# Mamba periods: D x by a diagonal on TensorE, the unscanned states' share ahead of the scans, the residual between GpSimd's products

## The chip, the cores and the metric

The kernel runs on one core of a Trainium2 chip. The metric is the device time of one execution in microseconds. The times shown are the median of three runs and their extremes; beside them stands one profiled execution, whose trace is what the profile is read from. VectorE, ScalarE, GpSimd, TensorE and SyncE are called DVE, ACT, POOL, PE and SP in the rows of the profile. Each has its own queue and works through it in order; semaphores tie the queues together.

## The reference

The input is `x`, 8 images of 128 channels by 64 x 64 pixels, in fp32. The first layer is a Mamba block over the 4096 pixels of each image, in order, with 256 inner channels and 16 states:

```
xz = x @ W_in;  xh, z = split(xz)
xh = silu(conv of two taps over the sequence(xh))
dt_low, B, C = split(xh @ W_x)               # 8, 16, 16
dt = softplus(dt_low @ W_dt + b_dt);  A = -exp(A_log)
h[t] = exp(dt[t] A) h[t-1] + dt[t] B[t] xh[t]          # per inner channel and state
y[t] = sum over states of h[t] C[t]  +  D xh[t]
y = (y * silu(z)) @ W_out
x = silu(group_norm(y)) + x
```

After it come a layer normalisation over the channels, a causal additive attention within each image (`exp` of a tanh score, divided by its sum), a second layer normalisation with a router over 64 experts, the experts themselves, and a scatter of their outputs. The change touches the Mamba block alone.

## The kernel before

The work is done in three stages, one after the other on the same core: the Mamba block (function `mamba`), the attention with the routing (`attend`), and the experts with the scatter (in `attend` too). The order of all instructions in `mamba` and `attend` is written out by hand: each engine runs its instructions in the order in which the program issues them. A semaphore wait of one instruction holds up all that stand behind it on its engine.

`mamba` cuts the sequences into chunks of 512 pixels, eight to an image, 64 in all (NC = 64, NCH = 8). The 256 inner channels are two halves of 128 partitions, so that most tiles are 128 x 2 x 512 ("pair") and most PSUM tiles 128 x 512 ("single"). Only NR = 3 of the 16 states are scanned. For the other 13 the decay is taken to be zero within a step, so that their share of y is dt xh times the sum of B C over these states: `over`. The flag that `vanish` collects tells afterwards whether that held; it did for these inputs.

The loop at line 525 runs over periods. In one period up to ten chunks are at work, each at its own stage: c1 is the chunk that is just projected, c2 has its step sizes computed, c3 is scanned, c4 is summed, gated, projected back and stored. Then eight more chunks pass, since the group norm of an image needs all of its chunks (`store`, line 420, calls `group_norm` for the last chunk of an image). c5 is normalised, c6 gets the residual added, c7 is turned to tokens by PE, c8 is layer-normalised and turned back, c9 gets the attention's vectors, c10 is saved to DRAM. Before, c6 to c10 are 12, 13, 14, 15 and 16 periods behind the newest chunk.

The steps that the change touches, by their lines before:

- `inputs` (345): five operations on DVE, each 128 x 1024. The first (L349) computes (u + 1) - 1 with a tensor_scalar; the next three (L350 to L352) correct the logarithm with it and give dt; L354 gives dx = dt xh.
- `over` (356): one matmul (L359) of the 16-row product B C with a matrix that has ones in the rows of the unscanned states, into a single PSUM tile, and L361 on DVE, which multiplies it with dx and so begins y.
- `drive` (L377): dx times B for one scanned state, on DVE. `scan` (L386): two scans of 512 on DVE, which read the decay `da` from PSUM. `outputs` (L392): the scanned state times C, for both halves, on GpSimd, into `hc`.
- `sums` (396): for each half three matmuls by the identity (L399) add up the three `hc`, and L403 on DVE adds the sum to y.
- `gated` (405): for each half y + xh D with D per partition (L408, a scalar_tensor_tensor), then times silu(z) (L411).
- `residual` (L443): o + x for one chunk, 128 x 512, on GpSimd.
- `turn` (L450, L452), `moments` (L456 to L466: the store of the turned chunk and its statistics), `tokens` (L473: four tensor_scalar of 128 x 128 on DVE, which read the turned chunk `tt` and write `tok`), `turn_back` (L482 to L485), `vectors` (L490 to L497).
- `back` (L416) and `store` (L425, L426): the projection back, its copy by ACT and its statistics on DVE.

[...]the tag "s" has two single tiles (used in turn by pbc, pdt, py, over, pt, pb, po and the group norm), px, pz and da take two each. pz is written by `gate` and by `vectors`. `tt` has one buffer. `o` has NCH + 3 = 11 buffers, `hc` 5, `hs` 4, `db` 3.

Of the kernel before, what the change touches and what calls it, by code (L numbers as in the profile page):

```python
# [9 lines left out]
F32 = mybir.dt.float32  # L10
AF = mybir.ActivationFunctionType
ALU = mybir.AluOpType
AX = mybir.AxisListType

P = 128
CH = 512
# [19 lines left out]
NR = 3  # L36
# [8 lines left out]
def fast_path(  # L45
# [24 lines left out]
    nc = tc.nc  # L70
    B = x.shape[0]
    L = x.shape[2] * x.shape[3]
    NCH = L // CH
    NB = L // P
    NQ = CH // P
    NC = B * NCH
# [4 lines left out]
    const = ctx.enter_context(tc.tile_pool(name="const", bufs=1))  # L81
# [3 lines left out]
    ident = const.tile([P, P], F32, name="ident")  # L85
# [21 lines left out]
    def halves(name, src):  # L107
        t = const.tile([P, 2], F32, name=name)
        nc.sync.dma_start(t, src.rearrange("(h p) -> p h", p=P))
        return t  # L110

    convb = halves("convb", conv_b)
    bdt = halves("bdt", b_dt)
    dskip = halves("dskip", D)

    aneg = const.tile([P, 2, NS], F32, name="aneg")
    nc.sync.dma_start(aneg, A_log.rearrange("(h p) n -> p h n", p=P))
# [5 lines left out]
    rest = const.tile([NS, P], F32, name="rest")  # L123
# [127 lines left out]
    def mamba(mw, small, psum):  # L251
# [5 lines left out]
        ch = [{} for _ in range(NC)]  # L257
        stats = {}

        def pair(tag, name, bufs):  # L260
            return mw.tile([P, 2, CH], F32, tag=tag, name=name, bufs=bufs)

        def single(name):
            return psum.tile([P, CH], F32, tag="s", bufs=2, name=name)

        def load(c):
            b, k = divmod(c, NCH)
            xt = ch[c]["x"] = mw.tile([P, 1 + CH], F32, tag="xt", bufs=3, name=f"xt{c}")
            if k == 0:
                nc.vector.memset(xt[:, 0:1], 0.0)  # L270
                nc.sync.dma_start(xt[:, 1:], xf[b, :, :CH])
            else:
                nc.sync.dma_start(xt, xf[b, :, k * CH - 1 : (k + 1) * CH])
# [67 lines left out]
        def logarithm(c):  # L341
            ln = ch[c]["ln"] = pair("ln", f"ln{c}", 1)
            nc.scalar.activation(ln, ch[c]["u"], AF.Ln, bias=1.0)

        def inputs(c):

            u, ln, dt = ch[c].pop("u"), ch[c].pop("ln"), ch[c]["dt"]
            w = pair("db", f"w{c}", 3)
            nc.vector.tensor_scalar(w, u, 1.0, -1.0, ALU.add, ALU.add)  # L349
            nc.vector.tensor_tensor(w, u, w, ALU.subtract)  # L350
            nc.vector.tensor_tensor(w, w, ln, ALU.add)
            nc.vector.tensor_tensor(dt, dt, w, ALU.add)  # L352
            dx = ch[c]["dx"] = pair("dx", f"dx{c}", 2)
            nc.vector.tensor_tensor(dx, dt, ch[c]["xc"], ALU.mult)  # L354

        def over(c):

            po = single(f"over{c}")
            nc.tensor.matmul(po, lhsT=rest, rhs=ch[c].pop("prod"), start=True, stop=True)  # L359
            y = ch[c]["y"] = pair("y", f"y{c}", 2)  # L360
            nc.vector.tensor_tensor(y, ch[c]["dx"], po.unsqueeze(1).to_broadcast([P, 2, CH]), ALU.mult)  # L361

        def vanish(c):
            for h in range(2):
# [30 lines left out]

        def sums(c, h):
            py = single(f"py{c}_{h}")
            for n in range(NR):
                nc.tensor.matmul(  # L399
                    py, lhsT=ident, rhs=ch[c]["hc", n][:, h, :], start=n == 0, stop=n == NR - 1  # L400
                )
            y = ch[c]["y"]
            nc.vector.tensor_tensor(y[:, h, :], y[:, h, :], py, ALU.add)  # L403

        def gated(c):
            y = ch[c]["y"]
            for h in range(2):
                nc.vector.scalar_tensor_tensor(  # L408
                    y[:, h, :], ch[c]["xc"][:, h, :], dskip[:, h : h + 1], y[:, h, :], ALU.mult, ALU.add
                )  # L410
            nc.vector.tensor_tensor(y, y, ch[c].pop("zs"), ALU.mult)  # L411

        def back(c):
# [6 lines left out]
        def store(c):  # L420
            b, k = divmod(c, NCH)
            if k == 0:
                stats[b] = small.tile([P, NCH, 6], F32, tag="gst", name=f"gst{b}")
            o = mw.tile([P, CH], F32, tag="o", bufs=NCH + 3, name=f"o{c}")
            nc.scalar.copy(o, ch[c].pop("pout"))  # L425
            nc.vector.bn_stats(stats[b][:, k, :], o)  # L426
            ch[c] = {key: v for key, v in ch[c].items() if key[0] == "hs"} | {"o": o}
            if k == NCH - 1:
                group_norm(b)
# [6 lines left out]
        def normal(c):  # L436

            b, o = c // NCH, ch[c]["o"]
            nc.scalar.activation(o, o, AF.Silu, bias=norm[:, b, 1:2], scale=norm[:, b, 0:1])
# [62 lines left out]
        def group_norm(b):  # L502
            mv = small.tile([P, 2], F32, tag="mv", name=f"gmv{b}")
            nc.vector.bn_aggr(mv, stats[b])
            pm = single(f"pm{b}")
            nc.tensor.matmul(pm[:, 0:1], lhsT=gmean, rhs=mv[:, 0:1], start=True, stop=True)
            sc = small.tile([P, 4], F32, tag="gsc", name=f"gsc{b}")

            nc.vector.tensor_copy(sc[:, 0:1], pm[:, 0:1])
            nc.vector.tensor_tensor(sc[:, 1:2], mv[:, 0:1], sc[:, 0:1], ALU.subtract)  # L510
            nc.vector.tensor_tensor(sc[:, 1:2], sc[:, 1:2], sc[:, 1:2], ALU.mult)
            nc.vector.tensor_tensor(sc[:, 1:2], sc[:, 1:2], mv[:, 1:2], ALU.add)
            pv = single(f"pv{b}")
            nc.tensor.matmul(pv[:, 0:1], lhsT=gmean, rhs=sc[:, 1:2], start=True, stop=True)
            nc.vector.tensor_scalar(sc[:, 2:3], pv[:, 0:1], EPS, None, ALU.add)
            nc.scalar.activation(sc[:, 2:3], sc[:, 2:3], AF.Ln)
            nc.scalar.activation(sc[:, 2:3], sc[:, 2:3], AF.Exp, scale=-0.5)
            nc.vector.tensor_tensor(norm[:, b, 0:1], sc[:, 2:3], gamma, ALU.mult)
            nc.vector.tensor_tensor(sc[:, 3:4], sc[:, 0:1], norm[:, b, 0:1], ALU.mult)
            nc.vector.tensor_tensor(norm[:, b, 1:2], beta, sc[:, 3:4], ALU.subtract)  # L520
# [1 line left out]
        load(0)  # L522
        load(1)
        nc.scalar.preload_act_table_set(LOG_EXP)
        for p in range(NC + NCH + 8):

            c1, c2, c3, c4, c5, c6, c7, c8, c9, c10 = (
                p - i if 0 <= p - i < NC else None
                for i in (0, 1, 2, 3, NCH + 3, NCH + 4, NCH + 5, NCH + 6, NCH + 7, NCH + 8)
            )  # L530

            def on(c, step, *args):
                if c is not None:
                    step(c, *args)

            if p + 2 < NC:
                load(p + 2)
            on(c5, again)
            on(c10, save)
            on(c6, residual)  # L540
            on(c3, decays, 0)
            on(c3, drive, 0)
            on(c3, drive, 1)
            on(c2, rows)
            on(c8, moments)
            on(c3, drive, 2)
            on(c1, project, 0)
            on(c2, steps)
            on(c2, magnitudes)
            on(c8, tokens)  # L550
            on(c1, project, 1)
            on(c3, scan, 0)
            on(c3, outputs, 0)
            on(c3, decays, 1)
            on(c2, logarithm)
            on(c3, scan, 1)
            on(c3, outputs, 1)
            on(c3, decays, 2)
            on(c4, sums, 0)
            on(c3, scan, 2)  # L560
            on(c3, outputs, 2)
            on(c4, sums, 1)
            on(c3, over)
            on(c3, vanish)
            on(c4, gated)
            on(c1, gate)
            on(c1, silus)

            if p < NC + 3:
                on(c5, normal)  # L570
            elif p == NC + 3:
                for c in range(NC - NCH, NC):
                    normal(c)
            if p <= NC + 3:
                nc.scalar.preload_act_table_set(LOG_EXP)
            on(c7, turn)
            on(c8, turn_back)
            on(c9, vectors)
            on(c4, back)
            on(c2, inputs)  # L580
            on(c4, store)


# [530 lines left out]
    with (  # L1114
        tc.tile_pool(name="mwork", bufs=1) as mw,
        tc.tile_pool(name="msmall", bufs=2) as small,
        tc.tile_pool(name="mpsum", bufs=1, space=bass.MemoryType.PSUM) as psum,
        tc.manual_schedule(),
    ):
        mamba(mw, small, psum)  # L1120
# [607 lines left out]
def conv_attn_hybrid_kernel(tc, *args):  # L1728
    W1, b1, w2, b2 = args[12:16]
    first = fractions_hold(tc, W1, b1, w2, b2)  # L1730
    second = fast_path(tc, *args)
    with tc.If(first + second < 2):
        general_path(tc, *args)
# [46 lines left out]
```

## Time and profile before

| what | us |
|---|---|
| median of 3 runs | 6327.22 |
| lowest, highest | 6325.18, 6329.36 |
| the profiled execution | 6327.88 |
| its span, first to last instruction | 6326.2 |

| engine | busy us in the span | share |
|---|---|---|
| PE | 5825.4 | 92% |
| ACT | 4987.7 | 79% |
| DVE | 4935.0 | 78% |
| POOL | 2023.4 | 32% |

A busy time is the sum of the times in which the engine had an instruction in work, and an instruction that waits for access to the memory counts as busy. "Idle before" is the time in which an engine waited for a semaphore. Row two of the page cuts the span into 40 slices of 158 us; the Mamba stage is the first twelve, and DVE is at 9 tenths in most of these, at 7 in the later ones, while PE goes from 8 to 9. The groups (line, engine, operation, shape, count, busy time and mean) and the timeline (start, duration, engine, line, operation, output and inputs) are the views used most below. The mean granted clock of PE was 0.946 over the span.

### The profile page before, as it was taken

The numbers are of one execution on the slowest core, as the hardware profiler recorded it, in microseconds if no ns is written. First come the engines' busy times: TensorE is split into PE (matmuls) and PEld (weight loads), VectorE is DVE, ScalarE is ACT, GpSimd is POOL, SyncE is SP. The second block draws the span as 40 slices with busy tenths as digits, with TensorE's granted clock in tenths as the row PEclk, the third lists the DMA queues.
The fourth block names the chain that finished last, engine by engine and source line by source line (L and its number), as shares of the span: only waits on it lengthen the run. The fifth ranks groups of instructions, "written<-read, shape, count | busy, mean of one in ns | idle before, by whom it ended". The sixth has DMA issues, their size and how long they took to land. (4 is left out here: it accounts for less than half of the span.)

```text
span 6326.2 us, 69220 instructions
## 1 busy us (share of the span) xinstructions
PE 5825.4 (92%) x22458; PEld 2224.5 (35%) x22458; DVE 4935.0 (78%) x7955; ACT 4987.7 (79%) x5657; POOL 2023.4 (32%) x1652
## 2 busy tenths in 40 slices
PE   7888888888869999999999999999999999999987
PEld 2333333333323333333333333333333333343335
DVE  7899999999956777777777777777777777777751
ACT  5667767767757998898899889889889988988941
POOL 2333333333312333333233233233333323323311
PEclk8888888888878999999999999999999999999989
DMA  2233333333341010101101101101100110110058
GB/s 81 74 110 117 125 122 126 122 127 127 115 145 60 24 44 26 32 12 49 29 24 32 37 21 44 34 24 31 38 21 24 40 38 24 32 34 24 15 190 303
DMA packets 182407, 426.64 MB, mean 67 GB/s; under 512 B 32579, under 2 KB 33235, under 8 KB 171283
## 3 DMA queue, kind: packets, MB, share of 16 engines
q1 hardware_dynamic: 172514, 403.48, 19.5%
q0 software_dynamic: 9376, 18.37, 0.8%
q8 instruction: 180, 2.95, 0.2%
q14 instruction: 193, 1.57, 0.1%
q10 hardware_dynamic: 144, 0.26, 0.0%
HBM read 295.12 MB, written 126.88 MB: 67 GB/s over the span
## 5 line engine op out<-in xcount | busy, mean ns | idle before, releaser
L624 PE MATMUL D<-U,V 32*128 32x512 f32 (+7 forms) x6912 | 2719.6, 606 | 15.6 <-DMA U<-uv_dram 13.3
L624 PE MATMUL N<-U,V 32*128 32x512 f32 (+7 forms) x6912 | 2354.7, 605 | 51.8 <-DVE mix L657 49.5
L659 POOL TENSOR_TENSOR mix<-mix 128x512 f32<-128x512 f32 (+1 forms) x1088 | 1350.0, 1241 | 2825.9 <-DVE mix L657 2702.7
L646 ACT ACTIVATE mix<-mix 128x2048 f32<-128x2048 f32 x973 | 1853.3, 1905 | 31.1
L671 DVE TENSOR_TENSOR mix<-mix,mix 128x512 f32<-128x512 f32 (+1 forms) x1088 | 736.5, 677 | 916.6 <-POOL mix L659 916.3
L643 ACT ACTIVATE mix<-D 128x1024 f32<-128x1024 f32 (+1 forms) x1088 | 1077.4, 990 | 440.2 <-PE N L624 391.7
L624 PEld LDWEIGHTS D<-U,V 32*128 32x128 f32 (+1 forms) x6912 | 879.4, 185 | 1420.0 <-issue 516.8
L657 DVE TENSOR_TENSOR mix<-mix,N 128x1024 f32<-128x1024 f32 (+1 forms) x1088 | 1284.2, 1180 | 29.5 <-PE N L624 22.8
L680 PE MATMUL av<-mix,tok 128*128 128x512 f32 (+3 forms) x2304 | 1208.9, 611 | 31.1 <-DVE sums L689 29.9
L624 PEld LDWEIGHTS N<-U,V 32*128 32x128 f32 (+1 forms) x6912 | 708.1, 184 | 274.0 <-DVE mix L657 237.5
L658 DVE TENSOR_TENSOR mix<-mix,N 128x512 f32<-128x512 f32 (+1 forms) x1088 | 722.0, 664 | 1.9 <-PE N L624 1.3
L644 ACT ACTIVATE mix<-D 128x512 f32<-128x512 f32 (+1 forms) x1088 | 632.3, 581 | 13.9 <-PE N L624 10.2
L680 PEld LDWEIGHTS av<-mix,tok 128*128 128x128 f32 x2304 | 350.8, 189 | 802.1 <-issue 691.1
L392 POOL TENSOR_TENSOR hc<-hs,rep 128x1024 f32<-128x1024 f32 x192 | 453.2, 2362 | 551.0 <-issue 377.4
L386 DVE TENSOR_TENSOR_SCAN hs<-da,hs,db 128x512 f32<-128x512 f32 x336 | 412.6, 1269 | 18.4 <-ACT da L373 10.0
L399 PE MATMUL py<-hc,ident 128*128 128x512 f32 x768 | 369.2, 633 | 0.9 <-ACT dt L337 0.9
L373 ACT ACTIVATE da<-dt,aneg 128x512 f32<-128x512 f32 x384 | 258.8, 687 | 122.8 <-DVE dt L352 79.9
L279 PE MATMUL px<-xt,wtap 128*128 128x512 f32 x512 | 346.7, 814 | 3.3 <-DMA xt<-in_x_dram 3.3
L326 PE MATMUL pdt<-bc,wdt 8*128 8x512 f32 x256 | 180.0, 824 | 138.7 <-DVE prod L320 85.8
L399 PEld LDWEIGHTS py<-hc,ident 128*128 128x128 f32 x768 | 166.7, 217 | 231.3 <-issue 219.8
L313 POOL DMA_DIRECT2D bc_dram<-bc x128 | 69.1, 544 | 512.8 <-ACT bc L311 512.8
L377 DVE TENSOR_TENSOR db<-dx,rep 128x1024 f32<-128x1024 f32 x192 | 228.0, 1215 | 0.1
(241 smaller groups left out, 5430.3 us busy)
## 6 DMA issues: line engine op xcount, KB each, us to landing
rep<-bc_dram SPq DMA_DIRECT2D x64, 1536.0 KB, 7.0
uv_dram<-uv SPq DMA_DIRECT2D x64, 768.0 KB, 3.5
xr<-in_x_dram SPq DMA_DIRECT2D x64, 256.0 KB, 3.3
k_dram<-tt SPq DMA_DIRECT2D x64, 256.0 KB, 7.2
k_dram<-tok SPq DMA_DIRECT2D x64, 256.0 KB, 7.3
U<-uv_dram SPq DMA_DIRECT2D x128, 128.0 KB, 2.9
V<-uv_dram SPq DMA_DIRECT2D x128, 128.0 KB, 2.9
U<-uv_dram SPq DMA_DIRECT2D x256, 64.0 KB, 2.0
```

Of the source, the lines that this page charges most:

```text
L386: nc.vector.tensor_tensor_scan(hs[:, h, :], ch[c].pop(("da", n, h)), db[:, h, :], first, ALU.mult, ALU.add)
L392: nc.gpsimd.tensor_tensor(hc, ch[c]["hs", n], ch[c]["rep"][:, 1, n, :].unsqueeze(1).to_broadcast([P, 2, CH]), ALU.mult)
L399: nc.tensor.matmul(py, lhsT=ident, rhs=ch[c]["hc", n][:, h, :], start=n == 0, stop=n == NR - 1)
L624: nc.tensor.matmul(t12[:, g - 1, at : at + n] if g else t0[:, at : at + n], lhsT=V[b, jb // NQ][r, ab, ts(jb % NQ, P)], rhs=U[b, ic][r, ab ...
L643: nc.scalar.activation(x[:, 1:3, lo:], d12[:, :, lo:], AF.Ln)
L644: nc.scalar.activation(x[:, 0, lo:], d0[:, lo:], AF.Ln)
L646: nc.scalar.activation(x[:, :, lo:], x[:, :, lo:], AF.Exp, scale=-1.0)
L657: nc.vector.tensor_tensor(r[:, 1:3, lo:], r[:, 1:3, lo:], n12[:, :, lo:], ALU.mult)
L658: nc.vector.tensor_tensor(r[:, 0, lo:], r[:, 0, lo:], n0[:, lo:], ALU.mult)
L659: nc.gpsimd.tensor_tensor(mix[k + 1][:, 3, lo:], r[:, 1, lo:], r[:, 2, lo:], ALU.add)
L671: nc.vector.tensor_tensor(s, s, mix[k - 2][:, 0, lo:], ALU.add)
L680: nc.tensor.matmul(av[0][:, q : q + n], lhsT=tok[b, jb // NQ][:, jb % NQ, :], rhs=mix[k + 1][:, 3, at : at + n], start=first, stop=last,)
```

## The change

D xh is no longer added by DVE. Ahead of the Mamba stage two diagonal matrices are built from the identity and D, one for each half, and `sums` begins each half's accumulation with a matmul of xh by that diagonal, in front of the three matmuls by the identity. `gated` is left with the multiplication by silu(z).

`over` is split. Its matmul, into a tile of the pz tag instead of s, is issued after the first half of `project` and before `steps`, and the multiplication with dx (now `others`) after `magnitudes`, ahead of the first scan, where `tokens` stood. L349 becomes a step of its own, `rounded`, which is issued after `vanish`, with `tokens` behind it and `gated` after both.

`residual` is issued between the first and the second of GpSimd's products with C, where it stood at the head of the period. `turn` takes its chunk in the same period as `residual`, later in the order, so that c7 to c10 are each one period earlier than before, the loop has one period less, and `o` has one buffer less.

```diff
+    skip = const.tile([P, 2, P], F32, name="skip")
     dskip = halves("dskip", D)
+    for h in range(2):
+        nc.vector.tensor_scalar(skip[:, h, :], ident, dskip[:, h : h + 1], None, ALU.mult)
...
+        def rounded(c):
+            w = ch[c]["w"] = pair("db", f"w{c}", 3)
+            nc.vector.tensor_scalar(w, ch[c]["u"], 1.0, -1.0, ALU.add, ALU.add)
+
         def inputs(c):
-            u, ln, dt = ch[c].pop("u"), ch[c].pop("ln"), ch[c]["dt"]
-            w = pair("db", f"w{c}", 3)
-            nc.vector.tensor_scalar(w, u, 1.0, -1.0, ALU.add, ALU.add)
+            u, ln, dt, w = ch[c].pop("u"), ch[c].pop("ln"), ch[c]["dt"], ch[c].pop("w")
             nc.vector.tensor_tensor(w, u, w, ALU.subtract)
...
         def over(c):
-            po = single(f"over{c}")
-            nc.tensor.matmul(po, lhsT=rest, rhs=ch[c].pop("prod"), start=True, stop=True)
+            ch[c]["over"] = psum.tile([P, 2, CH], F32, tag="pz", name=f"over{c}")[:, 0, :]
+            nc.tensor.matmul(ch[c]["over"], lhsT=rest, rhs=ch[c].pop("prod"), start=True, stop=True)
+
+        def others(c):
             y = ch[c]["y"] = pair("y", f"y{c}", 2)
-            nc.vector.tensor_tensor(y, ch[c]["dx"], po.unsqueeze(1).to_broadcast([P, 2, CH]), ALU.mult)
+            nc.vector.tensor_tensor(
+                y, ch[c]["dx"], ch[c].pop("over").unsqueeze(1).to_broadcast([P, 2, CH]), ALU.mult
+            )
...
         def sums(c, h):
             py = single(f"py{c}_{h}")
+            nc.tensor.matmul(py, lhsT=skip[:, h, :], rhs=ch[c]["xc"][:, h, :], start=True, stop=False)
             for n in range(NR):
-                nc.tensor.matmul(
-                    py, lhsT=ident, rhs=ch[c]["hc", n][:, h, :], start=n == 0, stop=n == NR - 1
-                )
+                nc.tensor.matmul(py, lhsT=ident, rhs=ch[c]["hc", n][:, h, :], start=False, stop=n == NR - 1)
...
         def gated(c):
             y = ch[c]["y"]
-            for h in range(2):
-                nc.vector.scalar_tensor_tensor(
-                    y[:, h, :], ch[c]["xc"][:, h, :], dskip[:, h : h + 1], y[:, h, :], ALU.mult, ALU.add
-                )
             nc.vector.tensor_tensor(y, y, ch[c].pop("zs"), ALU.mult)
...
-            o = mw.tile([P, CH], F32, tag="o", bufs=NCH + 3, name=f"o{c}")
+            o = mw.tile([P, CH], F32, tag="o", bufs=NCH + 2, name=f"o{c}")
...
-        for p in range(NC + NCH + 8):
+        for p in range(NC + NCH + 7):
...
-                for i in (0, 1, 2, 3, NCH + 3, NCH + 4, NCH + 5, NCH + 6, NCH + 7, NCH + 8)
+                for i in (0, 1, 2, 3, NCH + 3, NCH + 4, NCH + 4, NCH + 5, NCH + 6, NCH + 7)
...
             on(c10, save)
-            on(c6, residual)
             on(c3, decays, 0)
...
             on(c1, project, 0)
+            on(c3, over)
             on(c2, steps)
             on(c2, magnitudes)
-            on(c8, tokens)
+            on(c3, others)
             on(c1, project, 1)
             on(c3, scan, 0)
             on(c3, outputs, 0)
+            on(c6, residual)
             on(c3, decays, 1)
...
             on(c4, sums, 1)
-            on(c3, over)
             on(c3, vanish)
+            on(c2, rounded)
+            on(c8, tokens)
             on(c4, gated)
```

## The prediction

> **What bounds the kernel now.** First the table of busy time by stage, cut at landmarks of the timeline: from about 372 us on every step of a period is at work, the last chunk is being prepared until about 1746, the Mamba drain ends at 1902, the rest is attention and experts.
>
> ```profile
> 372.00:1746.00 1374.00, 1166.58 (x2496) 460.00 (x2494) 1316.49 (x1799) 968.46 (x1545) 493.72 (x348) 0.88 0.37 123
> 1902.00:6326.00 4424.00, 4274.61 (x19202) 1613.70 (x19202) 3229.12 (x5590) 3714.54 (x3638) 1381.50 (x1154) 0.98 0.14 47
> ```
>
> The columns are length, then PE, weight loads, DVE, ACT and POOL busy, granted clock, DMA. The last 4424 us are PE at 97%, and the change leaves them alone. In the full Mamba periods DVE is busy 1316 of 1374 us (96%), so a period lasts as long as DVE's list. But busy hides waiting. Here are one period's lines in the timeline (start, duration), VectorE first, then GpSimd, then TensorE.
>
> ```profile
> 777.17 5.05 DVE L386 TENSOR_TENSOR_SCAN hs<-da,hs,db 128x512 f32<-128x512 f32 x4
> 782.60 0.69 DVE L403 TENSOR_TENSOR y<-y,py 128x512 f32<-128x512 f32 x1 [0.38 <-PE py L399]
> 783.20 2.45 DVE L386 TENSOR_TENSOR_SCAN hs<-da,hs,db 128x512 f32<-128x512 f32 x2
> 785.57 0.66 DVE L403 TENSOR_TENSOR y<-y,py 128x512 f32<-128x512 f32 x1
> 786.22 1.22 DVE L361 TENSOR_TENSOR y<-dx,over 128x1024 f32<-128x1024 f32 x1
> 787.36 2.04 DVE L408 SCALAR_TENSOR_TENSOR y<-xc,dskip,y 128x512 f32<-128x512 f32 x2
> 789.43 1.23 DVE L411 TENSOR_TENSOR y<-y,zs 128x1024 f32<-128x1024 f32 x1
> 790.57 1.75 DVE L349 TENSOR_SCALAR w<-u 128x1024 f32<-128x1024 f32 x1
> ...
> 804.41 5.05 DVE L386 TENSOR_TENSOR_SCAN hs<-da,hs,db 128x512 f32<-128x512 f32 x4
> ```
>
> ```profile
> 779.76 2.37 POOL L392 TENSOR_TENSOR hc<-hs,rep 128x1024 f32<-128x1024 f32 x1 [7.66 <-issue]
> 782.36 2.37 POOL L392 TENSOR_TENSOR hc<-hs,rep 128x1024 f32<-128x1024 f32 x1 [0.23 <-DVE hs L386]
> 785.82 2.36 POOL L392 TENSOR_TENSOR hc<-hs,rep 128x1024 f32<-128x1024 f32 x1 [1.09 <-DVE hs L386]
> ...
> 789.94 1.84 POOL L443 TENSOR_TENSOR o<-o,xr 128x512 f32<-128x512 f32 x1 [0.80 <-ACT o L439]
> ```
>
> The period is 804.41 - 777.17 = 27.24 us. L408 starts at 787.36 and GpSimd's third product runs to 788.18: 0.82 us of L408's 2.04 is standing still. L349 starts at 790.57, the residual runs to 791.78, and L349 ends 0.54 later; with GpSimd idle it takes 0.68 (the minimum of its row), so 1.07 is a wait. L443 itself took 1.84 against its minimum of 1.26, as it waited for L411. The scans, L403 and L361, which read one operand from PSUM, run through GpSimd's products at their usual length. So a DVE operation that reads SBUF twice, or is a tensor_scalar from SBUF to SBUF, excludes a GpSimd product, and GpSimd gets its turn between two DVE operations. Per period, 0.82 + 1.07 of such waits and 0.38 for TensorE (L403) are in the 27.24.
>
> TensorE is the second reading: in windows of 3.41 us (start:end length, busy, clock) the clock halves once a period, a whole number of windows apart (800.8 and 828.1: 27.3, or 8).
>
> ```profile
> 797.35:800.76 3.41, 1.12 (x2) 1.00 0.02 4
> 800.76:804.17 3.41, 3.15 (x4) 0.50 0.88 223
> ...
> 807.58:811.00 3.42, 3.42 (x10) 1.00 0.24 87
> ```
>
> ```profile
> 803.01 3.78 PE L279 MATMUL px<-xt,wtap 128*128 128x512 f32 x4
> 806.59 5.82 PE L399 MATMUL py<-hc,ident 128*128 128x512 f32 x12
> ```
>
> The window before the drop held 1.12 us of work, of 8 rows (pdt); two windows ran at half clock. px took 3.78 instead of 1.88, and py came late: that is L403's wait.
>
> **The change part by part.**
>
> *D x on TensorE.* Both L408 go: one slot of 787.36 to 789.43, 2.07 us, of which 0.82 was the wait for the third product; only if that wait isn't met again by the next operation is it saved. Two matmuls of 128x512 come. py's 12 records (6 matmuls) take 5.31 at full clock, 0.885 a matmul, so +1.77 us of TensorE a period. They lie in front of both L403. In the period shown py0 was already 0.38 late.
>
> *The other states' share ahead of the scans.* L361 (1.14 in steps) moves, and the four tokens operations (L473, 1.14 by steps) move from in front of the scans to behind them: the sum of the two is unchanged. But L361 was the cover: it ran beside the third product. Behind the second L403 now stand rounded (the old L349), tokens and gated, and all have to exclude GpSimd. The matmul over goes from behind py to ahead of pdt, no cost in PE time (1.05 each way); its PSUM tile pz is free there, since the exponentials of puv have read it by 793.4.
>
> *The residual between the products.* L443 leaves the place where it delayed L349 (1.07). It now queues ahead of the second and third product on GpSimd. Counted from the first scan: first product starts at 2.59 (779.76 - 777.17), and then 2.37 + 1.26 + 2.37 + 2.36 back to back end at 10.95, 11.0 with issue. DVE is done with the second L403 at 5.03 + 0.60 + 2.37 + 0.65 = 8.65. So rounded (or tokens, if rounded slips in first) waits 2.3 us. The waits removed, 0.82 + 1.07, come back as one of 2.3.
>
> Here the Trainium skill, "SBUF — State Buffer", section on who interferes with whom, has a rule on what no row shows: tensor_scalar can take the pair shared with GpSimd, for the whole instruction. No tokens operation overlaps a GpSimd product in this trace. If tokens were free of it and rounded got in ahead of the third product, tokens would run beside it and the stall would be about 1.1 shorter. I take the rule: L349's row shows it for the same kind of operation.
>
> Sum for DVE: 27.24 - 2.07 - 1.07 - 0.38 + 2.3 = 26.0 us, if TensorE keeps up.
>
> *TensorE's side.* turn now is released by the residual (6.3) and follows pz; turn_back waits for tokens, behind the stall: rounded 11.0 to 11.65, first token at about 12.0. So TensorE stands still from about 9 to 12.1, then runs pb, puv and po, with no break, through pbc, px, over, pdt 0, pdt 1. The stored chunk is copied by 17.5, and its statistics are due on DVE at 18.9: covered by 1.4 us at full clock. The old gaps at po and pdt (0.61, 0.78, 1.86) close. TensorE at full clock then has 27.25 - 3.5 (gaps) - 3.2 (lost at half clock) = 20.5, plus 1.77 = 22.3 us of a 26.0 period.
>
> But does the clock hold? The Trainium skill, "TensorE: Matmul & The Clock Gate", Part 1, says that the clock halves after an idle window of 3.4 us. By that rule a gap of 3.1 hardly ever counts and the period is 26.0. The rows differ: a window with 1.12 us of pdt sufficed above; below, one with 2.05 us of work, all of it pdt, was followed by half clock, and one with only 1.29 us of full-row matmuls was not.
>
> ```profile
> 186.51:189.92 3.41, 1.29 (x3) 1.00 0.25 67
> ...
> 196.75:200.16 3.41, 2.05 (x4) 0.98 0.02 4
> 200.16:203.57 3.41, 3.41 (x5) 0.52 1.01 332
> ```
>
> So some 2.2 us of idleness or of matmuls of few rows in one window is enough. The change offers two such stretches: the gap before pb, and over, pdt, pdt (16 and 8 rows) now side by side, 3.2 us. I go by the rows: about one drop a period goes on. Worked at four positions of the windows: a drop at pb delays po by 0 to 0.2 if it lasts one window, 1.0 to 1.3 if two (covered but for about 0.1); a drop at pdt 1 (23.4 after the first scan) makes px end 1.8 into the next period, py0 with its four matmuls at 6.4 where DVE wants it at 5.03, the third scan 1.3 later and the third product's end at 11.7, +0.7; a drop late in px costs 0 to 0.2. Mean +0.4, period 26.4: a gain of 0.8 us.
>
> *The rest.* The 1374 us hold about 44 ordinary periods and 6 with a group norm: 44 x 0.8 = 35; the six have DVE idle on TensorE's answer anyway, and over stands in their cold stretch, so 0.5 each, 3. The pipeline is a period shorter: in the drain a period is set by the tt buffer's transfer,
>
> ```profile
> 1859.48 0.59 ACT L452 COPY tt<-pt 128x512 f32<-128x512 f32 x1 [4.01 <-DMA k_dram<-tt]
> ...
> 1866.76 0.59 ACT L452 COPY tt<-pt 128x512 f32<-128x512 f32 x1 [3.95 <-DMA k_dram<-tt]
> ```
>
> 7.3 us, and one of these goes. The first 372 us have neither tokens nor residual; the saved L408 meets the third product there too, and py is 0.85 to 2.2 late already: 0, from -5 to +5. The two tensor_scalar that build the diagonals cost about 0.6 (0.37 for the like L98, less overlap) ahead of the first chunk. o's ring of 10 is enough, since the slot was turned a period before; SP's order is as before but for the shift by one chunk. Sum: 35 + 3 + 7 - 0.6 = 45. Profiled time 6327.9 (span 6326.2) - 45 = 6283; the median of the runs, 6327.2, is within 1 us of that execution, so **6283 us**.
>
> **The rivals.** *More is won*: tokens or the products overlap better than I say, and the 2.3 stall shrinks. Then TensorE binds at 22.3 + 3.4 at half clock = 25.7, a gain of 1.5 x 50 + 7: 6245. For it: the naive list (2.07 + 1.07) promises more. Against: every two-SBUF operation in the trace waited. *The clock eats it*: TensorE's lost time keeps the period at 8 windows, 27.3, as it is now (the group norms' matmuls at 491.1 and 713.0 are 221.8 apart, 65 windows of 3.4125); only the drain is won: 6327.9 - 7 + 0.06 x 50 = 6324. *Slower*: both stretches drop the clock, and py0 and po are late in the same period. A two-window drop at pb delays the statistics by 1.0 to 1.6, and 0.7 at py0 adds to it: 26.0 + 1.6 = 27.6, +0.4 x 50 - 7 = +13: 6341. It decides from a mean delay of 1.35 us a period, where drain and periods cancel. Against: after a late py the gap before pb shrinks below 2.2, so the two rarely meet. That the change fails to do what it says is excluded by the order of instructions, which has every move.
>
> **How the numbers follow.** My case 0.56 (its own range 6260 to 6312), more 0.13, clock 0.15, slower 0.16. No change is within 0.2%, 12.7 us. Faster: 0.13 + 0.55 and a little of the clock case = 0.69; same 0.15; slower 0.16. The range reaches from the rival of more to that of slower, 6243 to 6338; the ends beyond hold 0.2.
>
> **What would show it.** No L408; rounded at 2 to 3 us in most periods, waiting on the third product; L443 at 1.26; group norms 213 to 217 us apart; L403 late by 0 to 1.4; clock drops still about one a period; drain some 94 us. If rounded is at 0.68 the lock reading is wrong; if DVE waits for the stored chunk's copy, the slower rival holds.

## The result, and the profile after

The changed kernel takes 6249.2 us (6242.0 to 6249.7 in four runs), beside 6328.3 (6325.2 to 6336.2) of the kernel before. The ratio estimated from the runs is 0.9871, with a 95% interval of 0.9859 to 0.9883. It is 79 us faster; 45 were forecast.

The profiled execution's span fell from 6326.2 to 6248.0 us, by 78.2. Landmarks of VectorE's timeline divide this. The first group norm (its `bn_aggr`) starts at 264.55 instead of 271.42: 6.9 us. From there to the eighth pass 1457.4 us instead of 1530.3: 72.9. From the eighth to the first load of the attention's vectors pass 93.9 instead of 100.0: 6.1. The rest takes 4432.1 instead of 4424.4: 7.7 lost. In the variants below, which leave that rest alone too, it took 4422.8 to 4437.1, so these 7.7 are within what it varies by. Small differences between variants are therefore given for the Mamba stage alone as well, up to that first load, from the profiled executions.

The stages of the changed kernel, columns as in the table before (length, then PE, weight loads, DVE, ACT and POOL busy, granted clock, DMA):

```profile
372.00:1680.00 1308.00, 1139.87 (x2699) 477.38 (x2700) 1261.80 (x1705) 972.89 (x1552) 472.22 (x350) 0.92 0.39 130
1816.00:6248.00 4432.00, 4284.70 (x19202) 1621.67 (x19202) 3229.27 (x5590) 3713.90 (x3638) 1379.53 (x1154) 0.98 0.15 46
```

VectorE is still busy 96% of the full periods. The granted clock rose from 0.88 to 0.92, although TensorE has more to do in a period. One period in the timeline, VectorE and then GpSimd:

```profile
798.71 5.04 DVE L396 TENSOR_TENSOR_SCAN hs<-da,hs,db 128x512 f32<-128x512 f32 x4
803.67 0.66 DVE L412 TENSOR_TENSOR y<-y,py 128x512 f32<-128x512 f32 x1
804.25 2.46 DVE L396 TENSOR_TENSOR_SCAN hs<-da,hs,db 128x512 f32<-128x512 f32 x2
806.61 0.67 DVE L412 TENSOR_TENSOR y<-y,py 128x512 f32<-128x512 f32 x1
807.19 2.86 DVE L351 TENSOR_SCALAR w<-u 128x1024 f32<-128x1024 f32 x1
809.98 1.10 DVE L478 TENSOR_SCALAR tok<-tt,lmv,rs 128x128 f32<-128x128 f32 x4
811.00 1.21 DVE L416 TENSOR_TENSOR y<-y,zs 128x1024 f32<-128x1024 f32 x1
...
817.31 0.69 DVE L431 BATCH_NORM_STATS2 gst<-o 128x6 f32<-128x512 f32 x1 [0.18 <-ACT o L430]
...
824.53 5.04 DVE L396 TENSOR_TENSOR_SCAN hs<-da,hs,db 128x512 f32<-128x512 f32 x4
```

```profile
801.29 2.35 POOL L402 TENSOR_TENSOR hc<-hs,rep 128x1024 f32<-128x1024 f32 x1 [7.77 <-issue]
803.61 1.27 POOL L448 TENSOR_TENSOR o<-o,xr 128x512 f32<-128x512 f32 x1
804.83 4.67 POOL L402 TENSOR_TENSOR hc<-hs,rep 128x1024 f32<-128x1024 f32 x2
```

The period shown is 824.53 - 798.71 = 25.82 us. The most frequent one is 25.56; the clock drops in it too, but delays nothing on VectorE. The products and the residual run back to back from 801.29 to 809.50, 10.79 after the first scan. L351 (`rounded`) starts at 807.19 and stands still until then: 2.86 us for an operation of 0.68. No L408 of before is left, and the residual takes its plain 1.27.

TensorE in the same period, and then its windows of 3.41 us (start:end length, busy, clock):

```profile
806.78 0.60 PE L455 MATMUL pt<-ident,o 128*128 128x128 f32 x4
810.37 1.10 PE L487 MATMUL pb<-ident,tok 128*128 128x128 f32 x4 [2.98 <-DVE tok L478]
811.30 3.03 PE L498 MATMUL puv<-xT,wuv 128*128 128x512 f32 x4
814.13 2.47 PE L421 MATMUL po<-y,wout 128*128 128x512 f32 x4
...
819.96 0.69 PE L364 MATMUL over<-prod,rest 16*128 16x512 f32 x1
819.97 0.69 PE L330 MATMUL pdt<-bc,wdt 8*128 8x512 f32 x1
820.50 0.59 PE L364 MATMUL over<-prod,rest 16*128 16x512 f32 x1
820.50 1.64 PE L330 MATMUL pdt<-bc,wdt 8*128 8x512 f32 x3
```

```profile
808.38:811.79 3.41, 1.42 (x6) 1.00 0.37 131
811.79:815.20 3.41, 3.41 (x6) 0.52 0.00 0
815.20:818.61 3.41, 3.41 (x9) 0.98 0.38 145
```

TensorE waits 2.98 us for the tokens behind the stall. The window with that wait is followed by one at half clock: puv takes 3.03 instead of 1.88, po is late, and VectorE waits 0.18 for the stored chunk at L431. That is where the clock drops most often now. Cutting 372 to 1680 us into 383 such windows, 63 show a clock below 0.6 ("half-clock windows" below); before it was 94. The clock's own records tell them apart. Before, there were 47 drops of two windows each, one a period, 41 behind pdt and six at a group norm. Now there are 52, still about one a period, but 40 of them last one window and only 12 last two; 34 stand at pb, 12 behind pdt and six at a group norm. So L412 waits less often for the sums. What VectorE idled before it in those 1308 us (us, times), in the kernel before and then in the changed one:

```profile
  PE py L399: 19.1, 40
```

```profile
  PE py L410: 7.1, 9
```

Measured by the start of `prod`, an ordinary period (one without a group norm) between 372 and 1640 us took 27.15 us on the mean before and takes 25.88 now; one with a group norm took 31.71 and takes 29.13.

### The profile page after: what moved, and what is told of

Read it like the earlier page. It is cut to its first block, busy times and chain, and to the rows that moved or that the text cites. A ratio compares the mean times of both kernels' runs of the same rounds, so it can differ in the third digit from the quotient of the medians.

```text
span 6248.0 us, 69479 instructions
## 1 busy us (share of the span) xinstructions
PE 5802.7 (93%) x22714; PEld 2254.2 (36%) x22714; DVE 4860.9 (78%) x7829; ACT 4986.9 (80%) x5657; POOL 1992.1 (32%) x1652
## 3 DMA queue, kind: packets, MB, share of 16 engines
q8 instruction: 182, 2.98, 0.2%
## 5 line engine op out<-in xcount | busy, mean ns | idle before, releaser
L631 PE MATMUL D<-U,V 32*128 32x512 f32 (+7 forms) x6912 | 2730.8, 607 | 16.6 <-DMA U<-uv_dram 13.3
L410 PE MATMUL py<-hc,ident 128*128 128x512 f32 x768 | 354.1, 597 | 0.0
L283 PE MATMUL px<-xt,wtap 128*128 128x512 f32 x512 | 288.2, 692 | 3.9 <-DMA xt<-in_x_dram 3.9
L410 PEld LDWEIGHTS py<-hc,ident 128*128 128x128 f32 x768 | 149.7, 195 | 193.7 <-issue 193.4
L487 PE MATMUL pb<-ident,tok 128*128 128x128 f32 x256 | 74.3, 386 | 153.4 <-DVE tok L478 153.4
```

The lines of the kernel that those rows point to most:

```text
L410: nc.tensor.matmul(py, lhsT=ident, rhs=ch[c]["hc", n][:, h, :], start=False, stop=n == NR - 1)
L631: nc.tensor.matmul(t12[:, g - 1, at : at + n] if g else t0[:, at : at + n], lhsT=V[b, jb // NQ][r, ab, ts(jb % NQ, P)], rhs=U[b, ic][r, ab ...
```

## The experiments

The change has three moves: D x on TensorE (D), the share ahead of the scans (S), the residual between the products (R). The variants were each measured beside the kernel before (6328.1, 6330.0 and 6326.0 us in the three series). The first are these:

| variant | us | ratio, 95% interval | ordinary period | half-clock windows of 383 |
|---|---|---|---|---|
| before | 6328.1 | 1 | 27.15 | 94 |
| S and R (e1) | 6327.9 | 0.9999, 0.9990 to 1.0007 | 27.01 | 100 |
| D (e2) | 6221.9 | 0.9828, 0.9812 to 0.9845 | 25.37 | 41 |
| D and R (e3) | 6205.9 | 0.9807, 0.9791 to 0.9824 | 25.11 | 42 |
| D and S (e4) | 6315.0 | 0.9978, 0.9970 to 0.9987 | 27.14 | 95 |
| D, S, R: the change | 6249.2 | 0.9871, 0.9859 to 0.9883 | 25.88 | 63 |

All but before have the pipeline that is a period shorter; their drain is 92.3 to 93.9 us instead of 100.1. D x alone gives more than the whole change. The move of the share is a loss: 43 us where the residual is moved, 93 where it isn't. The residual's move gains 16 us without the share's (e3 beside e2) and 66 with it.

**D x back on VectorE (e1).**

```diff
-            nc.tensor.matmul(py, lhsT=skip[:, h, :], rhs=ch[c]["xc"][:, h, :], start=True, stop=False)
...
+            for h in range(2):
+                nc.vector.scalar_tensor_tensor(y[:, h, :], ch[c]["xc"][:, h, :], dskip[:, h : h + 1], y[:, h, :], ALU.mult, ALU.add)
             nc.vector.tensor_tensor(y, y, ch[c].pop("zs"), ALU.mult)
```

> The changed kernel with D x back on VectorE (two scalar_tensor_tensor ahead of the gating product, no diagonal matmuls). Theory (VectorE's list with its waits for GpSimd sets the period): GpSimd's chain is over by then, so the two cost their plain 0.61 each, 1.25 a period, nothing is taken off the stall of rounded: some 27.1 us a period instead of 25.85, +62 over 50 periods: about 6311. Rival (TensorE, with its 22.3 of work and the time lost at half clock, sets the changed period): 1.77 of TensorE's work goes away and pays for VectorE's 1.25: 6225 to 6275.

It gave 6327.9. The period is 27.01, 1.45 longer than the changed kernel's most frequent 25.56. From VectorE's timeline:

```profile
790.60 2.87 DVE L347 TENSOR_SCALAR w<-u 128x1024 f32<-128x1024 f32 x1
...
794.42 1.40 DVE L414 SCALAR_TENSOR_TENSOR y<-xc,dskip,y 128x512 f32<-128x512 f32 x2
```

The stall is the same (2.87), so D x takes nothing off it; the pair costs 1.40 with GpSimd idle. TensorE's 1.77 fewer don't help (100 half-clock windows instead of 63), and VectorE never waits for the sums between 372 and 1680 us: its own list is the bound, and the rival falls. Of the 79 us, 15 lie ahead of the first group norm (279.87 instead of 264.55), which I had not counted. I had costed the pair from the pair of before, which took 2.04 in the row and of which I had called 0.82 a wait. It lost 2.04 - 1.40 = 0.64.

**D x alone (e2).**

```diff
+            nc.tensor.matmul(py, lhsT=skip[:, h, :], rhs=ch[c]["xc"][:, h, :], start=True, stop=False)
...
-                nc.vector.scalar_tensor_tensor(...)
...
-            o = mw.tile([P, CH], F32, tag="o", bufs=NCH + 3, name=f"o{c}")
+            o = mw.tile([P, CH], F32, tag="o", bufs=NCH + 2, name=f"o{c}")
...
-        for p in range(NC + NCH + 8):
+        for p in range(NC + NCH + 7):
```

> The kernel before with D x on TensorE alone (and, since the diagonals need the room, the ring of o at 10 with the pipeline a period shorter); share and residual as before. Theory (waits are passed on): the 0.82 that L408 waited for the third product is met by the gating product instead, and the wait of 1.07 for the residual stays; 1.25 is saved, some 0.4 is given back at the sums, whose matmuls are 1.77 longer: period 26.4, gain 0.8 x 50 + 6: about 6281. Rival (the waits belong to L408 and go with it): 2.07 a period and 6: about 6218. Rival (half clock keeps the period at eight windows, 27.3): about 6321.

It gave 6221.9, which is the time of the first rival, but not by its mechanism. One period's VectorE and GpSimd:

```profile
772.99 1.21 DVE L365 TENSOR_TENSOR y<-dx,over 128x1024 f32<-128x1024 f32 x1
774.12 1.99 DVE L410 TENSOR_TENSOR y<-y,zs 128x1024 f32<-128x1024 f32 x1
776.03 0.68 DVE L353 TENSOR_SCALAR w<-u 128x1024 f32<-128x1024 f32 x1
776.75 2.17 DVE L354 TENSOR_TENSOR w<-u,w 128x1024 f32<-128x1024 f32 x1
```

```profile
772.66 2.37 POOL L396 TENSOR_TENSOR hc<-hs,rep 128x1024 f32<-128x1024 f32 x1 [0.61 <-DVE hs L390]
775.03 0.10 POOL L484 MEMSET tok<- 128x4 f32 x1
776.11 1.72 POOL L442 TENSOR_TENSOR o<-o,xr 128x512 f32<-128x512 f32 x1 [0.98 <-ACT o L438]
```

In this period the waits were passed on as I expected: L410, the gating product, meets the third product (1.99 instead of 1.22), L354 meets the residual (2.17 instead of 1.23). So from 27.24: -2.07 for L408's slot, +0.77, -1.07 for the old L349's wait, +0.94, -0.38 for L403's wait makes 25.4; the mean is 25.37. About half of the ordinary periods look different, as this one, with a third product from 514.63 to 516.99:

```profile
514.71 0.69 DVE L406 TENSOR_TENSOR y<-y,py 128x512 f32<-128x512 f32 x1 [0.24 <-PE py L404]
515.76 1.22 DVE L365 TENSOR_TENSOR y<-dx,over 128x1024 f32<-128x1024 f32 x1 [0.36 <-PE over L363]
516.90 1.22 DVE L410 TENSOR_TENSOR y<-y,zs 128x1024 f32<-128x1024 f32 x1
...
520.01 2.17 DVE L355 TENSOR_TENSOR w<-w,ln 128x1024 f32<-128x1024 f32 x1
```

The second sum and the share wait 0.24 and 0.36 for TensorE, L410 then takes its plain 1.22, the residual meets L355, and the period is the same 25.25. So a wait for TensorE that was over before the third product cost nothing here. What failed in my expectation was the 0.4 that I let the longer sums give back; the wait of 0.38 at the first sum went away instead, with more than half of the half-clock windows.

**The share back behind the sums (e3).**

```diff
-            on(c3, over)
             on(c2, steps)
             on(c2, magnitudes)
-            on(c3, others)
...
             on(c4, sums, 1)
+            on(c3, over)
```

(`over` as before the change: in a single tile, with VectorE's product behind it.)

> The changed kernel with the other states' share back behind the sums (matmul and VectorE's product, in the pool of single tiles), rounded and tokens behind it. Theory (the stall of rounded is the exclusion between VectorE and GpSimd, and the share, with one operand in PSUM, runs beside the third product): the share's 1.14 covers as much of the stall, rounded at 1.3 to 1.8 instead of 2.4 to 2.9, period 24.7 instead of 25.85, -55: about 6195. Rival (TensorE already sets the changed period): no gain, 6240 to 6260, the time turning up as waits of L412 or L431 for TensorE.

It gave 6205.9. VectorE behind the sums, and GpSimd's third product:

```profile
789.69 0.69 DVE L408 TENSOR_TENSOR y<-y,py 128x512 f32<-128x512 f32 x1 [0.38 <-PE py L406]
790.75 1.22 DVE L367 TENSOR_TENSOR y<-dx,over 128x1024 f32<-128x1024 f32 x1 [0.36 <-PE over L365]
791.88 0.69 DVE L351 TENSOR_SCALAR w<-u 128x1024 f32<-128x1024 f32 x1
```

```profile
789.49 2.36 POOL L398 TENSOR_TENSOR hc<-hs,rep 128x1024 f32<-128x1024 f32 x1 [0.57 <-DVE hs L392]
```

L367, with one operand in PSUM, takes its usual 1.22 beside the third product, and when `rounded` starts the product is over. On the mean L351 takes 1.14 us (2.40 in the changed kernel, both over 600 to 900 us). That the stall is the exclusion, and that the share was its cover, is shown. The gain stays at 43 of the 55 expected, because part of the stall came back as other waits: 10.1 us in twelve periods for the decays from ScalarE, 4.0 for py and 1.8 for `over`.

**The residual at the head of the period (e4).**

```diff
             on(c10, save)
+            on(c6, residual)
...
-            on(c6, residual)
             on(c3, decays, 1)
```

> The changed kernel with the residual issued at the head of the period, as before the change. Theory: the third product ends when its scan lets it, at 10.4 instead of 10.8 after the first scan, so the stall of rounded is 0.4 shorter; but the residual then runs after the memset that waits for pb and excludes one of VectorE's products of two SBUF operands, +1.26: period about 26.7, +45: about 6294. Rival (only the length of GpSimd's chain behind the first scan counts): -0.4 a period, about 6230.

It gave 6315.0, 66 us more than the change. VectorE, and GpSimd's residual:

```profile
775.40 0.69 DVE L412 TENSOR_TENSOR y<-y,py 128x512 f32<-128x512 f32 x1 [1.31 <-PE py L410]
...
779.43 2.10 DVE L351 TENSOR_SCALAR w<-u 128x1024 f32<-128x1024 f32 x1
...
784.86 2.18 DVE L357 TENSOR_TENSOR w<-w,ln 128x1024 f32<-128x1024 f32 x1
```

```profile
783.10 2.85 POOL L448 TENSOR_TENSOR o<-o,xr 128x512 f32<-128x512 f32 x1
```

The conflict that I expected is there (L357 loses 0.95 to the residual), and so is one that I didn't: py0 is 1.31 late. The prediction had worked out what a drop behind pdt would do ("py0 with its four matmuls at 6.4 where DVE wants it at 5.03"); here it happens in most periods, 58 us of such waits in 70 of 94 sums. The group norms are 221.9 us apart, as in the kernel before, and so are 65 windows: the clock's records change in steps of 3.4133 us.

**Is it the clock?** That can be tested without touching VectorE's list: matmuls of all 128 rows in TensorE's idle places, into PSUM that the next real matmul overwrites. They add nothing to the result.

```diff
             pb = single(f"pb{c}")
+            for r in range(2):
+                for h in range(2):
+                    nc.tensor.matmul(pb[:, ts(h, 2 * P)], lhsT=ident, rhs=wtap[:, h, :], start=True, stop=True)
...
                 rows = slice(64 + 32 * h, 64 + 32 * h + DTR)
+                for r in range(2 * h * 2 if c + 1 < NC else 0):
+                    nc.tensor.matmul(ch[c + 1]["px"][:, 1, ts(r % 2, 2 * P)], lhsT=ident, rhs=wtap[:, r % 2, :], start=True, stop=True)
```

The first place is filled in e5 alone, the second in all three (in e5 with two matmuls instead of four).

> The changed kernel with idle places of TensorE filled: four matmuls of 256 columns ahead of pb's transposes (their result is overwritten by them) and two between pdt 0 and pdt 1 (overwritten by px). Theory (half clock costs the changed kernel what lies between its 25.55 and its mean of 25.88): the 63 half-clock windows of 383 fall to 10 or fewer and 0.33 x 43 is won: about 6235. Rival (TensorE's late results are hidden from VectorE): no change, 6249. Rival (the drop only moves, from in front of pb to in front of px, where py comes late): 6255 or more.

> The changed kernel with the residual at the head of the period (6315 in the run before) and four matmuls of 256 columns between pdt 0 and pdt 1. Theory (that variant is held at eight clock windows of 3.4125 a period by the drop behind pdt, which makes py late by 1.3): L412's wait of 1.33 a period goes, period 25.8 to 26.2 instead of 27.14, group norms no longer 221.9 apart: 6250 to 6275. Rival (what holds it there is the residual in VectorE's way, as I expected of that variant, 26.7): the filling saves at most 0.3 a period, 6300 to 6315.

> The kernel before with four matmuls of 256 columns between pdt 0 and pdt 1. Theory (the clock holds the period before at eight windows too; VectorE's own list with its waits for GpSimd is 26.85): L403's wait of 0.38 goes and the period with it: 26.85, group norms 219 apart, -17: about 6311. Rival (VectorE's waits alone make 27.25; half clock only uses up slack): 6328.

| variant | unfilled | filled | ratio to before, interval | ordinary period (unfilled) | group norms apart | half-clock windows |
|---|---|---|---|---|---|---|
| the change (e5) | 6249.2 | 6227.9 | 0.9836, 0.9819 to 0.9852 | 25.62 (25.88) | 205.4, then 208.2 | 25 |
| D and S (e6) | 6315.0 | 6271.9 | 0.9907, 0.9891 to 0.9924 | 26.48 (27.14) | 213.9 to 215.5 | 37 |
| before (e7) | 6330.0 | 6310.3 | 0.9966, 0.9955 to 0.9978 | 26.88 (27.15) | 218.3 to 219.2 | 13 |

The three theories held in the main: matmuls that do nothing for the result save 21, 43 and 20 us (in the Mamba stage of the profiled executions 17, 46 and 18). VectorE's waits for py between 372 and 1680 us fall from 7.1 to 3.4 us in e5, from 58.0 to 2.3 in e6 and from 19.1 to none in e7. So the clock delayed the kernel before and the D-and-S variant; with it out of the way the most frequent periods are 26.63 and 26.21. In e5 nearly all ordinary periods stand at 25.55 to 25.60. Two parts missed: e5 keeps 25 half-clock windows where at most 10 were expected, and e6's mean of 26.48 lies above its 25.8 to 26.2, since a few periods of 28 are left. Filled beside filled (e6 and e5, which is filled in front of pb too), the residual's place is still worth 44 us, so the larger part of its 66 doesn't seem to be the clock.

**A better order.** e3 left waits for the decays and for py. From e3 on, `prod` and the moments, which pdt 1 and ScalarE's queue wait for, can go ahead of the products with B: in e8 ahead of all three, in e9 behind the first. e10 is e9 with the matmuls ahead of pb; e11 is e3 with the filling at both places. The edit of e9, beside e3's:

```diff
             on(c3, drive, 0)
-            on(c3, drive, 1)
             on(c2, rows)
             on(c8, moments)
+            on(c3, drive, 1)
             on(c3, drive, 2)
```

> The changed kernel with the share back behind the sums (6206 in the run before), and prod and the moments ahead of the three products with B instead of between them. Theory (in that variant the decays come 0.79 late from ScalarE, which stands before the moments' result, and pdt 1 late because of prod): these waits go, some of the stall on the third product comes back: period 24.3 to 24.7 instead of 25.11, 6170 to 6190. Rival (TensorE with its half-clock windows sets 25.1): 6200 to 6210.

> The changed kernel with the share back behind the sums, and prod and the moments behind the first of the three products with B. Theory (with prod ahead of all three, it waited 1.02 for the copy of pbc; one product of 1.16 covers that, and the moments are still early enough for the decays): period 24.4 at full clock, up to 24.9 with the drop in front of pb: 6175 to 6195. Rival (the waits only go round: half clock in front of pb makes po and with it pbc late): 6200 to 6210.

> The same with four matmuls of 256 columns ahead of pb's transposes. Theory (what is left there is half clock behind TensorE's wait for the tokens): puv and po at full clock, pbc 0.9 earlier, period 24.4: 6165 to 6180. Rival (VectorE's list with the stall on the third product is all there is): as without the filling, within 5.

> The changed kernel with the share back behind the sums, prod and moments in their place, and the filling matmuls at both places (four ahead of pb, two between the pdt). Theory (of its 25.11, half clock costs some 0.3 as in the changed kernel): L408's waits for py go, the 0.79 for the decays stays: period 24.8, 6185 to 6195. Rival (TensorE is so nearly full, 22.3 plus 2.65 of filling, that it becomes the bound): 6206 or more.

| variant | us | ratio to before, interval | ordinary period |
|---|---|---|---|
| e8 | 6208.4 | 0.9808, 0.9792 to 0.9824 | 25.32 |
| e9 | 6170.1 | 0.9752, 0.9735 to 0.9768 | 24.53 |
| e10 | 6160.2 | 0.9734, 0.9718 to 0.9750 | 24.46 |
| e11 | 6195.6 | 0.9791, 0.9775 to 0.9808 | 25.17 |

e8 missed its 6170 to 6190 and lies where its rival had it, but not for the rival's reason. The decays came in time, and a new wait took their place, 51 us in 39 periods between 372 and 1640 us:

```profile
793.83 0.68 DVE L324 TENSOR_TENSOR prod<-bc,pbc 16x512 f32<-16x512 f32 x1 [1.02 <-ACT bc L315]
```

One product in front of `prod` covers this 1.02, and e9 gains 38 us over e8: the version that is faster than both kernels, 79 us below the change, with D x on TensorE and the residual between the products, and the share where it was. In it L351 is at 1.60 on the mean over 600 to 900 us, so some of the stall is back. e9 and e10 both came out 5 us below the ranges expected of them. e10's filling is worth 10 in the medians, 6 in the Mamba stage of the profiled executions. e11 gained 10 (the theory said 11 to 21). Most of its periods stand at the theory's 24.8, but the mean did not fall (25.17 beside 25.11), since the period behind each group norm now takes 26.3 to 26.9, where it took 24.8 to 25.6 in e3. Why isn't traced; that TensorE has become the bound isn't shown.

## Why the prediction was right or wrong

The measured 6249 lies in the whole range, but 11 us below the 6260 to 6312 that the prediction gave its own case: the mechanism was right, the gain of 45 too small by 34. That the range held the result is owed to a rival whose mechanism didn't come.

*The bound and the reading of the waits* were right. L408 is gone; the wait of the old L349 is gone (L448 at 1.27); the stall came up at `rounded`, where the sum had put it: 2.86 - 0.68 = 2.18 in the period shown, against 2.3. *That tokens are excluded as well*, taken from the Trainium skill ("SBUF — State Buffer", who interferes with whom), is now in the trace. In the first chunk of an image `rounded` slips in ahead of the third product, and tokens wait in its place (3.13 for four that take 1.10), from the changed kernel's timeline, VectorE and GpSimd:

```profile
673.39 1.05 DVE L351 TENSOR_SCALAR w<-u 128x1024 f32<-128x1024 f32 x1
674.36 3.13 DVE L478 TENSOR_SCALAR tok<-tt,lmv,rs 128x128 f32<-128x128 f32 x4
```

```profile
671.53 5.11 POOL L402 TENSOR_TENSOR hc<-hs,rep 128x1024 f32<-128x1024 f32 x2
```

*The sum of 26.0* was 0.44 too long; the most frequent period is 25.56. `rounded` ended 11.34 after the first scan instead of 11.65, since the chain ended at 10.79 and not at 11.0 and the operation needed 0.55 behind its release and not 0.65; tokens took 1.02 instead of 1.14 from start to start.

*The clock's 0.4* was about right: 25.88 - 25.56 = 0.32 on the mean, and e5, with 21 drops instead of 52, comes to 25.62. "About one drop a period" held. The rows were the better guide than the rule of a whole idle window: at all 34 drops at pb, TensorE had stood idle for 1.6 to 2.8 us of the 3.41 before. The price of a single drop was right where it lasts one window (0 to 0.26 on the period, with 0.18 at L431) and too low where it lasts two. In front of pb such a drop makes L431 wait 1.1 and the period 1.2 longer, where all but 0.1 was to be covered; behind pdt the period is 1.15 longer, where 0.7 was forecast. There are only four of each in the ordinary periods. The gap ahead of pb was there as forecast (2.98 against 3.1). The second stretch was shorter than its 3.2: over and pdt 0 ran side by side, and from 819.96 to pdt 1's end at 822.14 it is 2.2.

*Ordinary periods* therefore gained 1.27 and not 0.8, over 44 of them 21 us more. *The six with a group norm* gained 2.6 and not 0.5, 12 us more. Two terms beyond those of an ordinary period are in the timelines. In the first chunk of an image L403 waited 0.94 for TensorE and not 0.38, and L412 waits for nothing there: 0.56. And from `bn_aggr` to the next product with B, across two answers of TensorE, pass 3.3 to 3.5 instead of 3.72. The remaining 0.5 I haven't taken apart. *The first 372 us* gained 6.9 up to the first group norm, and I had 0 from -5 to +5. The step that failed there is "the saved L408 meets the third product there too". From 40 us to the first group norm, L408's 16.2 us are gone; only 11.8 came back, 9.8 at `rounded` (8.2 before, 18.0 now) and 2.0 at the subtraction behind it. The waits for the decays fell from 6.7 to 2.0. Those for py did not fall, they rose from 11.1 to 13.3, although the granted clock from 40 to 266 us went from 0.85 to 0.89. Together these four differences make the 6.9. Why the decays come earlier isn't traced. The waits in that stretch (us, times, longest), before and then after:

```profile
DVE y L403 <- PE py L399: 11.1, 8, 2.2
DVE hs L386 <- ACT da L373: 6.7, 8, 1.4
```

```profile
DVE y L412 <- PE py L410: 13.3, 15, 3.0
DVE hs L396 <- ACT da L383: 2.0, 4, 0.7
```

*The drain* gave 6.1 of the 7. Two of the signs failed: the group norms are 209.5 to 211.2 us apart and not 213 to 217, which goes with the larger gain, and VectorE does wait for the stored chunk's copy (7.2 us in 19 waits between 372 and 1680 us), which was to be the mark of the slower rival. The waits are there, but too small to make the kernel slower.

*The rivals.* The time is nearly that of "more is won" (6245), but the mechanism isn't: the stall hadn't shrunk, and TensorE didn't bind. "The clock eats it" describes the full periods of D and S without R, at 221.9 between group norms; with the residual moved as well, the change is not held there. The "slower" rival's two late places never met in the changed kernel.

What the prediction missed altogether is the share of each move. It said that the share "was the cover", and priced the stall that came of it, but worked out the change as one sum; a sum for each move would, by its own prices, have shown that S only loses. And it booked the 1.77 us of new matmuls as a risk to the clock, where the clock got better with D: e2 beside before has 41 half-clock windows instead of 94. Whether that is owed to the matmuls themselves or to VectorE's shorter list, which moves everything against the windows, is not separated; the filled variants show only that matmuls in idle places can do it.

## What to carry to other kernels

Cost each move of a change by itself and also with the others: here one move was worth more than all three, and undoing another gave 43 us. An operation that may run beside an engine's exclusive partner is cover; before moving it, ask what stands behind it then. And where a period, or a group of them, comes to a whole number of clock windows time after time, suspect that the clock sets it: a few matmuls in idle places, with no other effect, tell.

## What the runs showed of the hardware

- A period can be tied to the clock's window. Before, and with D and S, eight periods took 65 windows of 3.4133 us (221.9 us), group after group; four matmuls of 256 columns in the idle place in front of pdt 1 (1.9 us long in the period shown of before) undid it and saved 20 and 43 us. e5 and e8 come to 208.2, which is 61 windows; whether they are tied as well wasn't tried.
- Two matmuls of few rows on different rows of the array run at the same time: over (16 rows) and pdt 0 (8 rows) start at 819.96 and 819.97 and end together after 1.13 us, and so in all 49 periods looked at; over alone took 1.12 in e2 and e3. The Trainium skill, "TensorE: Matmul & The Clock Gate", Part 3, tells of such packing; here it came about only because the change put the two next to each other.
- An operation that waits for GpSimd didn't lose all of the time by which it overlapped GpSimd's: the pair L408 overlapped 0.82 and lost 0.64 (2.04 against 1.40 in e1), and `rounded` ended 0.55 after its release, where it takes 0.68.
